# Fused FFT-attention and Mamba layers on one core: the diagonals of B go through DRAM

## The chip, the core and the metric

The kernel runs on one core of a Trainium2 chip. The metric is the device time of one execution in microseconds (us); the result of a version is the median of several runs. The core has a matrix engine (PE, whose weight loads are listed as PEld), three other compute engines (DVE, ACT, POOL) and SP, which here only issues transfers. Transfers run on 16 DMA engines that all queues share.

## The reference

Two layers act on x of shape 8 x 128 x 128 x 128 (batch, channel, height, width). Layer 0, a block of FFT attention and convolutions, isn't touched by the change. Layer 1 is a selective state-space scan over the 16384 pixels of each image (`_gn` is a group norm):

```python
x = x + _L1_conv_ref(_gn(x), ...)

xz = u @ W_in                                  # u: pixels x 128 channels
xs, z = jnp.split(xz, 2, axis=-1)              # 256 inner channels each
xc = jax.nn.silu(depthwise causal conv of xs, 4 taps)
dt, Bm, Cm = jnp.split(xc @ W_xproj, [8, 24], axis=-1)   # 8, 16 and 16 columns
delta = jax.nn.softplus(dt @ W_dt + b_dt)
A = -jnp.exp(A_log)
def step(hs, inp):
    d_t, B_t, C_t, u_t = inp
    dA = jnp.exp(d_t[:, :, None] * A)
    h_new = dA * hs + (d_t * u_t)[:, :, None] * B_t[:, None, :]
    y_t = jnp.einsum('bdn,bn->bd', h_new, C_t)
    return (h_new, y_t)
y = ys + xc * D_param;  y = y * silu(z);  out = y @ W_out
```

Each image has 256 x 16 states (inner channel x state index n). For each pixel, a state is multiplied by dA and gets delta * xc * B added.

## The kernel before

Layer 0 runs first and leaves x1 in DRAM. After line 1020 the scan part follows. It cuts each image into 32 chunks of T = 512 pixels (`NCH`), 256 chunks in all, and each chunk into 16 steps (`ST`). One step handles 32 inner channels and, on the 128 partitions, 4 groups q of state indices; within a group two of the four indices m (`mp` says which pair) lie side by side. `where(n)` splits the step number n into chunk i, half h of the inner channels, pair mp and block k: steps 0 to 3 and 8 to 11 of a chunk use mp = 0, the others mp = 1.

A step passes four engines:

- `decay` (ACT): dA = exp(A * dlrep), twice, 128 x 512. `dlrep` holds the step sizes delta, repeated over the state groups. It is issued three steps ahead (`LEAD`).
- `product` (PE): hb = (delta * xc) * B for 128 rows and 2 x 512 columns, one step ahead, as 32 small matmuls. The weights are `duT`, the transposed delta * xc. The moving operand is `bd`: for each block j of 128 pixels, group q and pair mp a matrix that holds B on the diagonal of 64 pixels and zeros elsewhere, so that the matmul spreads the product over the pixels. hb lies in PSUM, with two buffers.
- `scan` (DVE): two tensor_tensor_scan over 512 pixels, reading dA and hb, writing `hs` (four buffers). ACT then copies the last column to `state` (`keep_state`).
- `weigh` (POOL): hc = hs * crep, where `crep` holds C repeated over 32 rows; `add` (PE) sums the groups into y.

Beside these, each chunk prepares the next ones. The list `beside` names, for every step, further pieces of work and the chunk that they are for (relative to i); `first` holds two that go ahead of the decay. They are the convolution and input projection (`conv`, `gate`, `xproj`), the step sizes (`step_sizes`, `step_sizes_act`), delta * xc (`drive`, on POOL) and its transpose (`turn`, `turn_act`), and the output (`skip`, `gated`, `project`, `residual`). `InOrder` holds PE, DVE, ACT and POOL to the order in which the program issues. SP's transfers aren't held so: the framework places them by its own estimate of when each is ready, and a transfer waits on SP, ahead of all that is issued later.

The columns of B take this way: `xproj_act` (step 5, for the next chunk) copies dt, B and C to `dbl`. `turn_b` (step 7) transposes the B rows on PE into a PSUM bank, so that pixels lie on the partitions; `keep_b` (step 8) copies them to `bt` on DVE. From step 11 on, `diagonals` makes a part of `bd` with one DVE product of `same` (an identity of 64, twice) and the transposed B, six such parts per chunk; `more_diagonals` makes the remaining 16 rows on ACT with `bt` as scale. `bd` has two buffers, one for each mp.

On SP, each chunk stores C (`cd`) to DRAM and reads it back repeated (`crep`, four transfers for each mp, `repeat_c`), and stores delta (`dld`) and reads it back repeated (`dlrep`, four transfers for each half h, line 1161). Every eighth chunk also loads an image block of 2 MB (`acc<-X`, `rows_of`) in pieces of 128 bytes, and ACT's queue stores one (`out<-acc`, `residual`).

Of the kernel before, what the change touches and what calls it, by code (L numbers as in the profile page):

```python
# [9 lines left out]
F32 = mybir.dt.float32  # L10
# [17 lines left out]
T = 512  # L28
# [83 lines left out]
def _layout(a):  # L112

    a = {n: np.asarray(v) for n, v in a.items()}
    o = {"x": np.ascontiguousarray(a["x"]).reshape(B, C, HW)}
    o["consts"], o["bconsts"], o["ker"] = _constants()
    p = "L0_conv_"
    f, s = a[p + "projf_w"].reshape(C, 2 * C), a[p + "projs_w"].reshape(C, 2 * C)

    rows = np.arange(C).reshape(2, 4, 16).transpose(1, 0, 2).reshape(-1)  # L120

    j, h = np.arange(8)[:, None], np.arange(NH)[None, :]
    frows = np.concatenate([(HD * h + j).reshape(-1), (HD * h + 15 - j).reshape(-1)])
    ws = [a[p + n + "1_w"].reshape(C, C) for n in "qkv"] + [f[:, frows], f[:, C:], s[:, rows], s[:, C:]]
    o["wpack"] = np.concatenate([w.T for w in ws] + [a[p + "w1"].reshape(NK, C).T], 1)
    tf = np.repeat(a[p + "temp_f"].reshape(NH), HD)
    ts = np.repeat(a[p + "temp_s"].reshape(NH), HD)[rows]
    o["cvec"] = np.stack([a[p + n + "1_b"] for n in "qkv"] + [tf, ts], 1)
    o["bn"] = np.concatenate([a[p + n] for n in ("b1", "bn_gamma", "bn_beta", "bn_mean", "bn_var")])[None]
    w2 = np.zeros((13, NK + 1, 13, C), np.float32)  # L130
    for u in range(13):
        w2[u, :NK, u] = a[p + "w2"].reshape(C, NK).T
        w2[u, NK, u] = a[p + "b2"]

    w2 = w2.reshape(13, NK + 1, 13, C // 8, 2, 4).transpose(0, 1, 4, 3, 5, 2)
    o["w2blk"] = w2.reshape(13 * (NK + 1), 13 * C)


    taps = np.zeros((4, NG, 2, 8, 8, 2, 4, 4), np.float32)
    for n, c in enumerate("qkvc"):  # L140
        for y in range(4):
            for x in range(4):
                taps[n, :, :, y + 1 : y + 4, x + 1 : x + 4, 0, y, x] = a[p + c + "3_w"]
                taps[n, :, :, y : y + 5, x : x + 5, 1, y, x] = a[p + c + "5_w"]
    taps = taps.reshape(4, NG // 4, 4, 2, 2, 4, 2, 4, 32)
    o["taps"] = taps.transpose(2, 3, 5, 7, 1, 0, 4, 6, 8).reshape(128, -1)
    p = "L1_conv_"
    o["win"] = a[p + "W_in"]
    o["cw"] = a[p + "conv_w"].T.reshape(1, 4 * DI)

    xp = a[p + "W_xproj"].reshape(2, 128, DR + 2 * DS).transpose(1, 0, 2)
    wx = np.zeros((128, 2, 4, 32), np.float32)
    wx[:, :, :2, :DR] = xp[:, :, None, :DR]
    wx[:, :, 2, :] = xp[:, :, DR:]
    o["wx"] = wx.reshape(128, 256)
    o["wdt"] = np.zeros((128, 128), np.float32)
    for h in range(2):
        o["wdt"][32 * h : 32 * h + DR] = a[p + "W_dt"][:, h * 128 : (h + 1) * 128]
    o["same64"] = np.tile(np.eye(64, dtype=np.float32), (2, 1))
    o["gath"] = np.tile(np.eye(32, dtype=np.float32), (4, 1))  # L160
    o["wout"] = a[p + "W_out"].reshape(2, 128, C).transpose(1, 0, 2).reshape(128, -1)
    halves = [a[p + n].reshape(2, 128).T for n in ("conv_b", "b_dt", "D_param")]
    o["dvec"] = np.concatenate(halves, 1)

    o["alog"] = a[p + "A_log"].reshape(DI // 32, 32, 4, 4).transpose(2, 1, 3, 0).reshape(128, -1)
    return {n: np.ascontiguousarray(v) for n, v in o.items()}
# [24 lines left out]
def tile_kernel(ctx: ExitStack, tc: tile.TileContext, I: dict, out: bass.AP):  # L191
# [830 lines left out]
    NQ, NM, NR, NBK = 4, 4, 32, DI // 32  # L1022
    ND, NTB = 64, T // 128
    QR = 32
    with tc.tile_pool(name="e_c", bufs=1) as cp, tc.tile_pool(name="e_w", bufs=2) as wk, tc.tile_pool(
        name="e_h", bufs=4
    ) as hp, tc.tile_pool(name="e_d", bufs=3, space=DRAM) as dp, tc.tile_pool(
        name="e_b", bufs=2, space=PSUM
# [4 lines left out]
            return t  # L1033

        gath = fixed("gath", [128, NR], I["gath"])
        same = fixed("same", [128, ND], I["same64"])
        unit = fixed("unit", [128, 128], I["consts"][:, 0:128])
        win = fixed("win", [128, 2 * DI], I["win"])
        wx = fixed("wx", [128, 2, 128], I["wx"])
        wdt = fixed("wdt", [128, 128], I["wdt"])  # L1040
        wout = fixed("wout", [128, 2, C], I["wout"])
# [3 lines left out]
        nc.scalar.activation(A, A, AF.Exp)  # L1045
        nc.vector.tensor_scalar(A, A, -1.0, None, ALU.mult)  # L1046

        wf = cp.tile([128, 4, DI], F32, name="wf")
        nc.sync.dma_start(wf.rearrange("p a d -> p (a d)"), I["cw"].partition_broadcast(128))
        for k in range(4):  # L1050
            nc.vector.tensor_tensor(wf[:, k, :], wf[:, k, :], win[:, 0:DI], ALU.mult)
        state = cp.tile([128, NM, NBK], F32, name="state")
        ch = {}
        total = B * NCH
        RT = T // W
# [3 lines left out]

        def load(i):  # L1060
            b, k = divmod(i, NCH)
            xin = wk.tile([128, T], F32, name="xin")
            nc.sync.dma_start(xin, X1[b, :, k * T : (k + 1) * T])
            ch[i] = {"xin": xin}

# [45 lines left out]
        def gate(i):  # L1111
            c = ch[i]
            c["sz"] = wk.tile([128, 2, T], F32, name="sz", bufs=3)
            for h in range(2):
                ps = bank("e_z", h)
                pe.matmul(ps, lhsT=win[:, DI + h * 128 : DI + (h + 1) * 128], rhs=c["u"][:, 3:], start=True, stop=True)
                act.activation(c["sz"][:, h, :], ps, AF.Silu)

        def xproj(i):
# [29 lines left out]
        def step_sizes_act(i):  # L1149
# [5 lines left out]
            nc.sync.dma_start(d.rearrange("h p t -> p h t"), c["dl"])  # L1155
            for h in range(2):
                if h:
                    repeat_c(i, 1)
                t = c["dlr", h] = wk.tile([128, 4, T], F32, name="dlrep")
                for q in range(NQ):  # L1160
                    nc.sync.dma_start(t[q * NR : (q + 1) * NR], d[h].rearrange("(k r) t -> r k t", r=NR))
# [29 lines left out]
                pe.transpose(c["bp"][:, 32 * j : 32 * j + 32], c["dbl"][rs, j * 128 : (j + 1) * 128], unit[rs, rs])  # L1191

        def keep_b(i):
            c = ch[i]
            c["bt"] = wk.tile([128, NTB, DS], F32, name="bt")
            dve.tensor_copy(c["bt"], c["bp"][:, : NTB * 32].rearrange("p (j n) -> p j n", n=32)[:, :, :DS])

        def diagonals(i, mp, j):


            c = ch[i]
            if (mp, j) in ((0, 0), (1, 0)):
                c["bd", mp] = wk.tile([128, NTB, NQ, ND, 2], F32, name="bd")
            to = [128, NQ, ND, 2]
            b = c["bp"][:, 32 * j : 32 * j + DS].rearrange("p (q m) -> p q m", m=NM)[:, :, 2 * mp : 2 * mp + 2]
            dve.tensor_tensor(
                c["bd", mp][:, j], same.unsqueeze(1).unsqueeze(3).to_broadcast(to), b.unsqueeze(2).to_broadcast(to), ALU.mult
            )

        def more_diagonals(i, which):  # L1210

            c = ch[i]
            for n in which:
                j, q, m = 2 + n // 8, n // 2 % 4, n % 2
                at = NM * q + 2 + m
                act.activation(c["bd", 1][:, j, q, :, m], same, AF.Identity, scale=c["bt"][:, j, at : at + 1])


        ST = 16
# [11 lines left out]
        def decay(n):  # L1231
            i, h, mp, k = where(n)
            for j in range(2):
                dA = hp.tile([128, T], F32, name="dA", bufs=10)
                kk = 4 * h + k
                act.activation(dA, ch[i]["dlr", h][:, k, :], AF.Exp, scale=A[:, 2 * mp + j, kk : kk + 1])
                dAs[n, j] = dA
# [69 lines left out]
        def residual(i):  # L1307
# [10 lines left out]

        beside = [
            (0, 1, lambda i: conv(i, 1, 2)),  # L1320
            (0, 0, lambda i: diagonals(i, 1, 1)),
            (0, 0, lambda i: more_diagonals(i, range(6, 11))),
            (1, 1, lambda i: conv(i, 1, 3)),
            (1, 0, lambda i: more_diagonals(i, range(11, 16))),
            (2, 1, conv_act),
            (2, -1, lambda i: add(i, 3, 0, 1)),
            (3, -1, lambda i: skip(i, 1)),
# [2 lines left out]
            (5, 1, xproj_act),  # L1330
            (5, 0, lambda i: add(i, 0, 0)),
            (6, 0, lambda i: add(i, 0, 1)),
            (6, 1, step_sizes),
            (6, 2, norm),
            (7, 1, turn_b),
            (8, -1, project),
            (8, 1, lambda i: drive(i, 0)),
            (8, 1, keep_b),
            (9, -1, residual),
            (9, 1, lambda i: drive(i, 1)),  # L1340
            (9, 2, lambda i: conv(i, 0, 0)),
            (10, 0, lambda i: add(i, 1, 0, 1)),
            (11, 0, lambda i: skip(i, 0)),
            (11, 1, lambda i: diagonals(i, 0, 0)),
            (11, 1, lambda i: turn(i, 0)),
            (11, 2, lambda i: conv(i, 0, 1)),
            (12, 0, lambda i: gated(i, 0)),
            (12, 1, lambda i: turn_act(i, 0)),
            (12, 1, lambda i: diagonals(i, 0, 1)),
            (12, 2, lambda i: conv(i, 0, 2)),  # L1350
            (13, 1, lambda i: diagonals(i, 0, 2)),
            (13, 1, lambda i: turn(i, 1)),
            (13, 2, lambda i: conv(i, 0, 3)),
            (14, 1, lambda i: turn_act(i, 1)),
            (14, 1, lambda i: diagonals(i, 0, 3)),
            (14, 0, lambda i: add(i, 2, 0, 1)),
            (15, 1, lambda i: diagonals(i, 1, 0)),
            (15, 1, lambda i: more_diagonals(i, range(6))),
            (15, 2, lambda i: conv(i, 1, 0, 1)),
        ]  # L1360
        first = [
# [46 lines left out]
```

## Time and profile before

| | before |
|---|---|
| median of 3 runs | 18559.42 us (18539.3 to 18562.05) |
| profiled execution | 18481.4 us, its span 18479.6 us |
| mean granted clock of PE | 0.958 |
| busy PE, DVE, POOL, ACT | 89%, 77%, 71%, 65% of the span |
| SP's hardware queue | 1730850 packets, 2206 MB, 43.9% of 16 engines |
| scans (DVE) | 1269 ns each |
| hc (POOL) | 2377 ns each |
| dA (ACT) | 714 ns each |

The shares are means over layer 0 (the first 14 of 40 slices) and the scan part (the rest), which have little in common. A row of a group gives engine, operation, output<-inputs, shapes and count; behind the first bar its busy time and the mean duration of one in ns; behind the second the idle time ahead of it and what ended that. In a row of SP's timeline the columns are start, time that the issuing took, queue, line, operation, transfer and count. In a row of waits they are engine, tile, what it waited for, us in total, number of times and the longest.

### The profile page before, as it was taken

The numbers are of one execution on the slowest core, as the hardware profiler recorded it, in microseconds if no ns is written. First come the engines' busy times: TensorE is split into PE (matmuls) and PEld (weight loads), VectorE is DVE, ScalarE is ACT, GpSimd is POOL, SyncE is SP. The second block draws the span as 40 slices with busy tenths as digits, with TensorE's granted clock in tenths as the row PEclk, the third lists the DMA queues.
The fourth block names the chain that finished last, engine by engine and source line by source line (L and its number), as shares of the span: only waits on it lengthen the run. The fifth ranks groups of instructions, "written<-read, shape, count | busy, mean of one in ns | idle before, by whom it ended". The sixth has DMA issues, their size and how long they took to land.

```text
span 18479.6 us, 790974 instructions
## 1 busy us (share of the span) xinstructions
PE 16503.3 (89%) x353336; PEld 9529.9 (52%) x353336; DVE 14244.2 (77%) x15987; ACT 12009.6 (65%) x26077; POOL 13090.9 (71%) x7572
## 2 busy tenths in 40 slices
PE   7789988888888889999999999999999999999998
PEld 5566665566555544444444444444444444444444
DVE  5544544334444479999999999999999999999999
ACT  4443434334233358778778878888888878887887
POOL 3333334444222269999999999999999989998998
PEclk8889999988999999999999999999999999999999
DMA  9963337777776654444454445444544454445443
GB/s 375 371 235 89 96 106 248 240 230 218 207 204 192 186 139 100 103 96 100 97 105 101 100 96 108 99 99 98 106 98 99 100 103 100 99 98 105 98 98 88
DMA packets 2434566, 2601.34 MB, mean 141 GB/s; under 512 B 1221965, under 2 KB 1624013, under 8 KB 2396866
## 3 DMA queue, kind: packets, MB, share of 16 engines
q1 hardware_dynamic: 1730850, 2206.28, 43.9%
q10 hardware_dynamic: 679840, 277.32, 7.1%
q0 software_dynamic: 20480, 67.13, 1.1%
q8 instruction: 2783, 45.60, 1.1%
q14 instruction: 613, 5.02, 0.1%
HBM read 1715.23 MB, written 834.93 MB: 138 GB/s over the span
## 4 chain that ended last, share of the span: by engine, by line
PE 56%; DVE 22%; DMA 8%; issue 7%; ACT 6%; POOL 1%; SPq 1%; DVEq 0%; ACTq 0%; POOLq 0%
DVE hs L180 15%; PE hb L180 14%; PE y L180 8%; PE c_mm L180 6%; PE e_xc L180 4%; DVE bd L180 3%; PE e_z L180 3%; PE e_x L180 3%; PE d_b L180 2%; PE a_mm L180 2%; DMA d_of<-OFL 2%; PE c_gram L180 2%; PE d_p L180 2%; DMA X<-d_x 2%; ACT L180 2%
## 5 line engine op out<-in xcount | busy, mean ns | idle before, releaser
L180 POOL TENSOR_TENSOR hc<-hs,crep 128x1024 f32<-128x1024 f32 x4096 | 9653.4, 2377 | 982.4 <-DVE hs L180 858.1
L180 DVE TENSOR_TENSOR_SCAN hs<-dA,state,hb 128x512 f32<-128x512 f32 x7936 | 9611.4, 1269 | 558.2 <-PE hb L180 418.8
L180 PEld LDWEIGHTS hb<-bd,duT 64*32 64x32 f32 x262144 | 3727.5, 106 | 3971.3 <-issue 2808.4
L180 PE MATMUL hb<-bd,duT 64*32 64x128 f32 x262144 | 4919.3, 275 | 798.9 <-issue 417.8
L180 ACT ACTIVATE dA<-dlrep,A 128x512 f32<-128x512 f32 x8192 | 5443.8, 714 | 59.6 <-DMA dlrep<-dld 51.6
L180 PE MATMUL e_xc<-u,wf 128*128 128x512 f32 x4096 | 2263.9, 646 | 34.1 <-DVE A L1046 20.8
L180 PE MATMUL y<-hc,gath 128*32 128x512 f32 x16384 | 2053.4, 601 | 32.5 <-issue 31.2
L180 ACT COPY state<-hs 128x2 f32<-128x2 f32 x4096 | 775.9, 189 | 1676.2 <-DVE hs L180 1649.5
L180 ACT ACT_TABLE_LOAD x1057 | 1356.1, 1283 | 75.0 <-PE e_dt L180 40.1
L180 PE MATMUL c_mm<-src,taps 32*32 32x512 f32 x32768 | 1211.5, 626 | 191.8 <-issue 158.7
L180 DVE COPY vst<-c_mm 128x512 f32<-128x512 f32 x1024 | 685.0, 689 | 717.4 <-PE c_mm L180 620.6
L180 ACT ACTIVATE bd<-same,bt 128x64 f32<-128x64 f32 x4096 | 1054.0, 339 | 0.8 <-PE hb L180 0.8
L180 DVE TENSOR_TENSOR bd<-same,e_bt 128x512 f32<-128x512 f32 x1536 | 1036.7, 675 | 0.0
L180 PEld LDWEIGHTS c_mm<-src,taps 32*32 32x32 f32 x32768 | 681.2, 105 | 683.7 <-issue 493.5
L180 POOL TENSOR_SCALAR qm<-vst,cst 128x512 f32<-128x512 f32 x256 | 505.4, 2070 | 745.4 <-DVE vst L180 745.2
L180 ACT ACTIVATE junk<-vst 128x256 f32<-128x256 f32 x1024 | 416.4, 410 | 923.0 <-DVE vst L180 921.9
L180 PE MATMUL a_mm<-xt,wp 128*128 128x256 f32 x3072 | 760.6, 409 | 264.5 <-ACT pk L180 184.1
L180 POOL TENSOR_TENSOR eo<-eo,et 128x1008 f32<-128x1008 f32 x128 | 298.8, 2334 | 969.3 <-DVE et L180 960.8
L180 POOL DMA_DIRECT2D X<-d_x x256 | 139.1, 543 | 1069.5 <-DVE d_x L180 939.9
L180 PEld LDWEIGHTS e_xc<-u,wf 128*128 128x128 f32 x4096 | 654.7, 194 | 440.2 <-issue 436.1
L180 DVE TENSOR_TENSOR d_x<-d_p,d_x 128x512 f32<-128x512 f32 x256 | 274.9, 1074 | 780.3 <-DMA d_x<-in_x 490.0
L180 PEld LDWEIGHTS a_mm<-xt,wp 128*128 128x128 f32 x3072 | 619.3, 205 | 421.7 <-ACT pk L180 194.6
(179 smaller groups left out, 20011.2 us busy)
## 6 DMA issues: line engine op xcount, KB each, us to landing
dlrep<-dld SPq DMA_DIRECT2D x2048, 256.0 KB
crep<-cd SPq DMA_DIRECT2D x2048, 128.0 KB
dld<-dl SPq DMA_DIRECT2D x256, 512.0 KB
src<-Pq SPq DMA_DIRECT2D x128, 544.5 KB
src<-Pv SPq DMA_DIRECT2D x128, 544.5 KB
src<-Pk SPq DMA_DIRECT2D x128, 544.5 KB
src<-Px SPq DMA_DIRECT2D x128, 544.5 KB
xt<-in_x SPq DMA_DIRECT2D x64, 1024.0 KB
```

What stands on the lines that cost most here:

```text
L180: made = method(*args, **kwargs)
```

## The change

`bd` is no longer made by DVE and ACT. At the start of the scan part four DRAM buffers (`diag`, two for alternating chunks times two for mp, 1 MB each) are filled with zeros from a zeroed tile. `keep_b`, now in step 6 and on ACT, copies the transposed B to `bt` and issues four transfers on SP, each of which writes 64 x 16 pieces of two numbers (8 bytes) from `bt` onto the diagonals of the DRAM buffers; the zeros between stay. `load_b` reads a whole buffer of 1 MB back as `bd`. Both loads of a chunk are issued in `step_sizes_act`, after the four repeats of the first half of the step sizes, ahead of `crep` of mp = 1 and the second half. `bd` has three buffers now. To make room, the first half of `win` is kept only until `wf` is made from it, `xin` has one buffer, and `dA` nine instead of ten. `turn_b` moves from step 7 to step 6, ahead of `step_sizes`.

```diff
+    cp = ctx.enter_context(tc.tile_pool(name="e_c", bufs=1))
+    wf = cp.tile([128, 4, DI], F32, name="wf")
+    nc.sync.dma_start(wf.rearrange("p a d -> p (a d)"), I["cw"].partition_broadcast(128))
+    DROW = NTB * NQ * ND * 2
+    diag = {(n, mp): dram.tile([128, DROW], F32, name=f"diag{n}{mp}") for n in range(2) for mp in range(2)}
+    with tc.tile_pool(name="e_0", bufs=1) as zp:
+        win_x = zp.tile([128, DI], F32, name="win_x")
+        nc.sync.dma_start(win_x, I["win"][:, 0:DI])
+        for k in range(4):
+            nc.vector.tensor_tensor(wf[:, k, :], wf[:, k, :], win_x, ALU.mult)
+        zero = zp.tile([128, DROW], F32, name="zero")
+        nc.gpsimd.memset(zero, 0.0)
+        for d in diag.values():
+            nc.sync.dma_start(d, zero)
...
-            xin = wk.tile([128, T], F32, name="xin")
+            xin = wk.tile([128, T], F32, name="xin", bufs=1)
...
             for h in range(2):
                 if h:
+                    load_b(i, 0)
+                    load_b(i, 1)
                     repeat_c(i, 1)
                 t = c["dlr", h] = wk.tile([128, 4, T], F32, name="dlrep")
...
         def keep_b(i):
             c = ch[i]
-            c["bt"] = wk.tile([128, NTB, DS], F32, name="bt")
-            dve.tensor_copy(c["bt"], c["bp"][:, : NTB * 32].rearrange("p (j n) -> p j n", n=32)[:, :, :DS])
-        def diagonals(i, mp, j):
...
-        def more_diagonals(i, which):
...
+            bt = wk.tile([128, NTB, DS], F32, name="bt")
+            act.copy(bt, c.pop("bp")[:, : NTB * 32].rearrange("p (j n) -> p j n", n=32)[:, :, :DS])
+            for mp in range(2):
+                d = diag[i % 2, mp]
+                for x in range(2):
+                    ap = [[DROW + 2, ND], [2 * ND, NTB * NQ], [1, 2]]
+                    to = bass.AP(d.tensor, d.offset + x * ND * DROW, ap)
+                    frm = bt[ND * x : ND * x + ND].rearrange("p j (q m) -> p (j q) m", m=NM)[:, :, 2 * mp : 2 * mp + 2]
+                    nc.sync.dma_start(to, frm)
+
+        def load_b(i, mp):
+            t = ch[i]["bd", mp] = wk.tile([128, NTB, NQ, ND, 2], F32, name="bd", bufs=3)
+            nc.sync.dma_start(t.rearrange("p j q t m -> p (j q t m)"), diag[i % 2, mp])
...
-                dA = hp.tile([128, T], F32, name="dA", bufs=10)
+                dA = hp.tile([128, T], F32, name="dA", bufs=9)
...
         beside = [
-            (0, 0, lambda i: diagonals(i, 1, 1)),
-            (0, 0, lambda i: more_diagonals(i, range(6, 11))),
-            (1, 0, lambda i: more_diagonals(i, range(11, 16))),
...
+            (6, 1, turn_b),
             (6, 1, step_sizes),
+            (6, 1, keep_b),
             (6, 2, norm),
-            (7, 1, turn_b),
-            (8, 1, keep_b),
...
-            (11, 1, lambda i: diagonals(i, 0, 0)),
-            (12, 1, lambda i: diagonals(i, 0, 1)),
-            (13, 1, lambda i: diagonals(i, 0, 2)),
-            (14, 1, lambda i: diagonals(i, 0, 3)),
-            (15, 1, lambda i: diagonals(i, 1, 0)),
-            (15, 1, lambda i: more_diagonals(i, range(6))),
```

## The prediction

> **What bounds the kernel now.** I read the page's slices first: from slice 16 on (the scan part, about 11.9 of 18.5 ms) DVE, PE and POOL all stand at 9 tenths, so no single busy share names the bound. The change touches only this part, so I then read one ordinary chunk and one disturbed one. The timeline of SP's queue cuts the chunks: the store of the step sizes (`dld<-dl`) goes out once per chunk.
>
> ```profile
> 10109.19 0.78 SPq L1131 DMA_DIRECT2D cd<-dbl  x2
> 10111.23 0.34 SPq L1063 DMA_DIRECT2D xin<-X  x1
> 10111.74 2.17 SPq L1140 DMA_DIRECT2D crep<-cd  x4
> 10114.01 0.38 SPq L1155 DMA_DIRECT2D dld<-dl  x1
> 10117.56 1.74 SPq L1161 DMA_DIRECT2D dlrep<-dld  x4
> 10126.23 1.71 SPq L1140 DMA_DIRECT2D crep<-cd  x4
> 10128.03 2.65 SPq L1161 DMA_DIRECT2D dlrep<-dld  x4
> ```
>
> The next `dld<-dl` stands at 10159.22: 45.2 us. Over all 256 chunks this distance is mostly 44.6 to 45.2, except every eighth, in which an image block of 2 MB is stored and the next one loaded in 128-byte pieces: 10338.47 to 10390.52, 52.1 us. So 224 ordinary chunks and 32 block chunks. The stretches of both:
>
> ```profile
> 10109.00:10154.00 45.00, 42.08 (x1136) 22.02 (x1136) 44.03 (x43) 37.30 (x81) 42.84 (x21) 1.00 0.36 92
> 10338.00:10390.00 52.00, 43.56 (x1123) 22.50 (x1130) 43.87 (x42) 37.05 (x80) 42.17 (x21) 0.97 1.03 162
> ```
>
> Columns: length, busy PE, PEld, DVE, ACT, POOL, granted clock, DMA share, GB/s. In the ordinary chunk DVE is busy 44.0 of 45.0 and sets the pace; but POOL (42.8) and PE (42.1) are only 1.2 and 2.0 behind. In the block chunk the engines do the same work and 7 us are lost. The groups between 10 and 14 ms (86.5 chunks) price the work, and PE's waits in the two stretches say what it lacks:
>
> ```profile
> L180 DVE TENSOR_TENSOR_SCAN hs<-dA,state,hb 128x512 f32<-128x512 f32 x2704 | 3273.8, 1268 | 195.2 <-PE hb L180 146.8 <-ACT bd L180 17.6 <-POOL hc L180 13.1
> L180 POOL TENSOR_TENSOR hc<-hs,crep 128x1024 f32<-128x1024 f32 x1383 | 3259.5, 2377 | 329.4 <-DVE hs L180 281.0 <-DMA dlrep<-dld 14.2 <-PE e_z L180 11.1
> L180 PE MATMUL hb<-bd,duT 64*32 64x128 f32 x88576 | 1663.1, 275 | 262.3 <-issue 143.2 <-DVE hs L180 117.0
> L180 ACT ACTIVATE bd<-same,bt 128x64 f32<-128x64 f32 x1376 | 354.0, 339 | 0.0
> L180 DVE TENSOR_TENSOR bd<-same,e_bt 128x512 f32<-128x512 f32 x516 | 347.3, 673 | 0.0
> ```
>
> ```profile
> PE hb L180 <- DVE hs L180: 1.2, 2, 0.7
> PE hb L180 <- issue: 1.2, 1, 1.2
> PE e_o L180 <- ACT dl L180: 0.5, 1, 0.5
> ...
> PE hb L180 <- issue: 4.2, 3, 2.6
> PE y L180 <- issue: 2.8, 1, 2.8
> ```
>
> The first three are the ordinary chunk, the last two the block chunk. "Issue" is time in which PE waited for nothing that the profile shows. It is 1.2 us in the one and 7.0 in the other, and the DMA share is what differs (0.36 against 1.03). In the block chunk the two long stalls begin, within 0.2 us, when a 16 KB packet of the instruction queue is under way. I read them as instruction fetches delayed by traffic; that reading is inferred.
>
> **What goes.** Per chunk six DVE products (6 x 0.673 = 4.0 us) and DVE's copy of bt (0.2); 16 ACT diagonals (16 x 0.339 = 5.4). DVE falls to 44.0 - 4.2 = 39.8 us of need and stops being the bound; ACT was not one. What is late next: POOL needs 42.8. PE needs 42.1 + 0.5 (e_o on ACT) + its issue stalls; with the 1.2 of today, 43.8. So PE, not POOL, comes next, and at unchanged stalls an ordinary chunk gains the 1.2 us that PE now waits for DVE, no more.
>
> A rule of the Trainium skill speaks against taking PE so: Perfetto Trace Analysis, Identifying the Most-Contended Engine, holds matmul busy time a poor measure of PE's headroom and asks for the share of weight loads; the row gives 22.02 of 45 us, under half. By that rule PE has room, POOL's 42.8 binds, and the 224 ordinary chunks could give 2.2 us each, some 490 us. I go by PE's timeline, which between 10126 and 10134 shows back-to-back matmuls.
>
> **What comes, on PE.** Two loads of 1 MB in 8 KB pieces. The first 30 us of the kernel, loads and stores of such pieces, moved 12.17 MB at 97.3% of the engines: 2.1 MB are 5.0 us. Four writes of 1024 pieces of 8 bytes, 256 pieces per DMA engine. No row has 8-byte pieces; the nearest are the 128-byte ones:
>
> ```profile
> q10 hardware_dynamic: 16400, 2.10, 62.4%
> ...
> q1 hardware_dynamic: 16310, 2.43, 155.1%
> ```
>
> The block store: 62.4% of 16 engines for 25 us over 16400 packets, 15.2 ns; the block load: 155.1% over 16 us, 24.3 ns (overlapping). Far ends: half of 15.2, and the 70 ns of the mean packet of SP's queue (39.6% over 4000 us, 362592 packets). I take 15.2, the write to DRAM: 3.9 us per chunk (2 to 18). The Trainium skill (DMA: Bandwidth & Descriptors, Measured) has 10.5 ns per packet in a minimum-size transfer; by it the writes would be 2.7 us, an estimate that no run here shows.
>
> Stalls per us of DMA time: ordinary 1.2 per 16.2 (0.07); the excess of the block chunk 5.8 per 37.4 (0.16). At these rates the additions cost 5.0 x 0.07 + 3.9 x 0.16 = 1.0 us more stall, nearly the whole 1.2. A stall beside another wait costs nothing, so I take 0.8: an ordinary chunk gains 0.4 us (bounds: 1.2 gained with no added stall, 0.3 lost with pieces at 24 ns and more stall per piece). 224 x -0.4 = **-90 us**.
>
> **What comes, on SP and the step sizes.** In the built order SP now issues cd, crep, the four diagonal writes, dld, the first diagonal load, the first-half dlrep, the second load, crep, the second-half dlrep. So the first load stands ahead of both halves, and its wait for the first two writes to land holds up the first half. With t0 the cd issue: crep is issued to 4.2, the writes add 4 x 0.43 = 1.7, dld goes at about 6.0 (now 4.8). Its data stand behind the small pieces, which start about 0.7 after their first issue: 5.3 + 3.9 + 1.3 = 10.5, seen at 11.7 (1.2 of latency, an estimate: today's 3.55 from dld to dlrep, less 0.38 to issue and 1.3 to move, leaves 1.9 for both ends). dlrep is issued then (now 8.4), its four issues take 1.74, its data go behind the load's 2.5 us and have landed about t0 + 17. It is needed by dA of the next chunk at 10126.72, t0 + 17.5; really late only when PE lacks duT, which ACT makes 3.4 us later, for the product at 10132.74: t0 + 20.1. So 3 us to spare, gone at 27 ns per small piece; beyond that each further 10 ns adds 2.6 us to every chunk. At 15.2 ns: nothing.
>
> The diagonals themselves are needed at t0 + 23.5 and land by about 14. The second load waits for PE's last product of step 11, but the crep behind it waits for POOL's step 11 anyway, and what follows is used 6 steps later: nothing. One xin buffer (freed 10 steps before), nine dA (ACT waits for the same scan's state copy first), e_bt ahead of e_dt on PE and the bt copy on ACT (0.4 and 0.2 us, inside the spare): nothing.
>
> **The block chunk.** The block store starts at t0 + 9.0 and holds half of every engine for 15.6 us. Already now ACT waits 2.2 us there for dlrep, to t0 + 19.7, and is saved by the spare. After: issue 3.3 later plus the load's 2.5 us at half rate, 8.3 later in all: t0 + 28, 7.9 too late; part of that falls into stalls that are there anyway. I take +6.5 (0 to 10): 32 x 6.5 = **+208 us**.
>
> **The start.** 4 MB of zeros and a memset go ahead of the constants: 4.2 MB at 12.17 MB per 29.2 us is 10 us, while the first block load, 16 us, moves behind the first xin. +10 (-10 to +30).
>
> **Sum**: -90 + 208 + 10 = +128 on the profiled execution's own 18481.4 us. The median of the runs shown, 18559.4, is 78 above that; with the same difference 18,690 us.
>
> **Rivals.**
> 1. Faster: the instruction fetches do not mind the new traffic, ACT's lead of three steps hides the late dlrep. For it: DVE alone holds the pace in ordinary chunks. Against it: 7 us of stall in the block chunk. Price: 224 x -1.0 + 32 x 2 + 0 = -160 to 18,400; with POOL the only bound 18,070.
> 2. Much slower: the 8-byte pieces take 40 ns and the first load blocks SP. Place: dlrep of the first half, every chunk; it decides from 27 ns on. Price: arrival 6.3 later, 3.3 too late; 224 x 2.9 + 32 x 12.5 + 10 = +1060, 19,620. For it: these are the smallest pieces of the kernel; against it: both 128-byte rows lie below 27.
> 3. No change: gain and losses cancel, 18,560; the sum's three terms are of one size, so this is thin but real.
>
> **Chances.** My forecast, slower by 0.2 to 2% (18,600 to 18,930), 0.36; slower than that, with rival 2 at its end, 0.24; rival 1 0.31; rival 3 0.09. A difference under 0.2% can't be told from none here. The range leaves out the POOL-bound end and pieces beyond about 37 ns: 18,300 to 19,500.
>
> **What would show it.** DVE's bd group gone and DVE near 88% of an ordinary chunk; PE's issue waits up from 1.2 to about 2 us per chunk; dlrep issued 3 us later after cd than now; block chunks at 58 us instead of 52. Wrong if SP waits long at the first load (rival 2: ACT waits for dlrep in every chunk), or if ordinary chunks come out below 44 us (rival 1).

## The result and the profile after

| | before | after |
|---|---|---|
| median of 4 runs each | 18549.36 us | 19732.94 us (19723.83 to 19737.89) |
| ratio | 1 | 1.064, 95% interval 1.0622 to 1.0658 |
| span of the profiled execution | 18479.6 us | 19722.0 us |
| mean granted clock of PE | 0.958 | 0.938 |
| ordinary chunk, mean | 45.42 us | 49.90 us |
| block chunk, mean | 52.33 us | 59.45 us |
| SP's hardware queue, share of 16 engines | 43.9% | 56.9% |

The kernel is 6.4% slower; 0.7% was forecast. The place is clear: 224 ordinary chunks x 4.48 us = 1003 us, 32 block chunks x 7.12 = 228, and the first `dld<-dl` comes 16 us later. These add to 1247 us; the spans differ by 1242.

SP's timeline of one ordinary chunk after the change:

```profile
10120.02 0.78 SPq L1141 DMA_DIRECT2D cd<-dbl  x2
10121.98 1.72 SPq L1150 DMA_DIRECT2D crep<-cd  x4
10123.79 3.79 SPq L1217 DMA_DIRECT2D diag<-bt  x4
10127.68 0.60 SPq L1165 DMA_DIRECT2D dld<-dl  x1
10130.06 0.34 SPq L1221 DMA_DIRECT2D bd<-diag  x1
10134.04 1.76 SPq L1173 DMA_DIRECT2D dlrep<-dld  x4
10136.23 1.24 SPq L1221 DMA_DIRECT2D bd<-diag  x1
10137.52 2.10 SPq L1150 DMA_DIRECT2D crep<-cd  x4
10140.64 6.57 SPq L1173 DMA_DIRECT2D dlrep<-dld  x4
```

The four diagonal writes occupy SP for 3.79 us (1.7 were forecast), so `dld` goes out 7.7 us after `cd`, and the first half of the repeats 14.0 us after it. The next `cd<-dbl` is at 10169.27. The stretch of this chunk, with the columns of the stretches shown before (length, busy PE, PEld, DVE, ACT, POOL, granted clock, DMA share, GB/s):

```profile
10120.00:10169.00 49.00, 43.21 (x1136) 22.59 (x1131) 40.40 (x36) 32.73 (x64) 42.14 (x21) 0.97 0.59 128
```

DVE is down to 40.4 us as forecast, and it bought nothing: no engine is now busy for more than 43.2 of 49 us. The waits of the same stretch say what took its place:

```profile
DVE hs L179 <- PE hb L179: 7.9, 4, 3.4
ACT dA L179 <- DMA dlrep<-dld: 6.2, 1, 6.2
PE hb L179 <- issue: 4.8, 3, 2.3
...
PE e_o L179 <- ACT dl L179: 1.0, 1, 1.0
```

DVE now waits for PE's products. ACT waits 6.2 us for the repeated step sizes. PE waits 4.8 us, in three stalls, for nothing that the profile's semaphores show; it was 1.2. Below, such a wait is called an issue stall. The groups between 10 and 14 ms (78.3 chunks after, 86.4 before) show that this is the rule:

```profile
L179 DVE TENSOR_TENSOR_SCAN hs<-dA,state,hb 128x512 f32<-128x512 f32 x2436 | 2940.8, 1264 | 797.5 <-PE hb L179 558.3 <-ACT dA L179 146.5 <-POOL hc L179 31.5
L179 ACT ACTIVATE dA<-dlrep,A 128x512 f32<-128x512 f32 x2502 | 1660.2, 714 | 590.3 <-DMA dlrep<-dld 588.4
L179 PE MATMUL hb<-bd,duT 64*32 64x128 f32 x79968 | 1587.9, 281 | 416.3 <-issue 302.2 <-ACT duT L179 98.9 <-DVE hs L179 7.8
L179 PE MATMUL y<-hc,gath 128*32 128x512 f32 x4992 | 667.5, 629 | 34.5 <-issue 34.5
```

PE's wait for DVE went from 117.0 to 7.8 us in 4 ms, so the change took away what it set out to take away. "Issue" went from 143.2 to 302.2, a wait for `duT` (98.9) is new, and ACT's wait for `dlrep` is 588.4 where it was 14.7.

Some of PE's stalls cost more than their length. PE's timeline, with the wait in brackets:

```profile
10140.90 1.16 PE L179 MATMUL hb<-bd,duT 64*32 64x128 f32 x64
10141.99 1.92 PE L179 MATMUL y<-hc,gath 128*32 128x512 f32 x16
10146.17 1.70 PE L179 MATMUL hb<-bd,duT 64*32 64x128 f32 x64 [2.26 <-issue]
10147.80 3.04 PE L179 MATMUL e_xc<-u,wf 128*128 128x512 f32 x4
```

After a stall of 2.26 us the same 64 products take 1.70 us instead of 1.16. The stretches of the stall and behind it say why (the seventh column is the granted clock):

```profile
10144.00:10146.00 2.00, 0.00 (x0) 0.00 (x0) 0.67 (x1) 2.00 (x5) 2.00 (x2) 1.00 1.02 186
10146.20:10149.60 3.40, 3.40 (x66) 2.05 (x66) 1.58 (x2) 2.69 (x7) 1.29 (x1) 0.55 1.06 225
```

The granted clock halves for one stretch of 3.4 us. Over the scan part the clock stands at one half for 1256 us, before for 367; half of that time is counted as lost. Of the 1256 us, 846 follow issue stalls (311 before) and 362 follow waits of PE for `duT` (none before).

The packets of the instruction queue in the trace tell what ends the issue stalls. After the change PE has 437 of them over 1 us in the scan part, and 96% end 1.2 to 1.8 us after a 16 KB packet of that queue has ended; 10% of moments picked at random do, and 3% of PE's waits for `dl`. Before the change it is 99% of 194. So PE waits there for its next instructions. The packets take hardly longer than before (1.17 us on average, 1.15 before) but come late: the one that ends such a stall starts 7.6 us after the one ahead of it, where the median of all is 5.4.

The bill per chunk, averaged over all (46.28 us before, 51.09 after, +4.81), from the waits of PE in these 4 ms and the half-clock time of the whole scan part:

| on PE, us per chunk | before | after | |
|---|---|---|---|
| issue stalls (hb, y, e_xc) | 1.84 | 4.39 | +2.55 |
| half of the half-clock time (367 and 1256 us over 256 chunks) | 0.72 | 2.45 | +1.73 |
| hb waits for `duT` | 0 | 1.26 | +1.26 |
| e_o waits for `dl` | 0.42 | 0.89 | +0.47 |
| hb waits for DVE | 1.35 | 0.10 | -1.25 |
| sum | | | +4.76 |

(`e_o` is the output product; it uses a PSUM bank that ACT frees by reading it into `dl`, the step sizes delta. `duT` comes from ACT too, in order behind the dA.) The five lines make up nearly all of the 4.81 us. PE's own busy time bears out the second: 42.6 us per chunk before, 44.4 after.

### The profile page after: what moved, and what is told of

It reads as the page before. It is cut to its first block, busy times and chain, and to the rows that moved or that the text cites. A ratio compares the mean times of both kernels' runs of the same rounds, so it can differ in the third digit from the quotient of the medians.

```text
span 19722.0 us, 787877 instructions
## 1 busy us (share of the span) xinstructions
PE 16953.1 (86%) x353336; PEld 9662.7 (49%) x353336; DVE 13418.0 (68%) x14195; ACT 10974.1 (56%) x22237; POOL 13070.1 (66%) x7573
## 3 DMA queue, kind: packets, MB, share of 16 engines
q1 hardware_dynamic: 2870114, 2755.80, 56.9%
## 4 chain that ended last, share of the span: by engine, by line
PE 63%; DMA 15%; ACT 9%; issue 7%; DVE 4%; SPq 1%; POOL 1%; ACTq 0%; DVEq 0%; POOLq 0%; another core or an unknown queue 0%
PE hb L179 17%; PE e_xc L179 9%; PE y L179 8%; PE c_mm L179 6%; DMA dlrep<-dld 5%; DMA dld<-dl 4%; ACT dA L179 3%; PE e_z L179 2%; PE e_x L179 2%; DMA d_of<-OFL 2%; ACT L179 2%; PE d_b L179 2%; PE a_mm L179 2%; PE d_p L179 2%; PE c_gram L179 2%
## 5 line engine op out<-in xcount | busy, mean ns | idle before, releaser
L179 PE MATMUL hb<-bd,duT 64*32 64x128 f32 x262144 | 5201.8, 280 | 1376.8 <-issue 990.4
L179 PEld LDWEIGHTS hb<-bd,duT 64*32 64x32 f32 x262144 | 3864.0, 108 | 4778.0 <-issue 3106.9
L179 PE MATMUL e_xc<-u,wf 128*128 128x512 f32 x4096 | 2412.6, 685 | 50.0 <-issue 31.1
L179 PE MATMUL y<-hc,gath 128*32 128x512 f32 x16384 | 2168.0, 623 | 110.1 <-issue 108.6
L179 PEld LDWEIGHTS e_xc<-u,wf 128*128 128x128 f32 x4096 | 701.4, 207 | 524.1 <-issue 520.9
L179 PEld LDWEIGHTS y<-hc,gath 128*32 128x32 f32 x16384 | 426.6, 111 | 903.1 <-issue 850.1
```

What stands on the lines that cost most here:

```text
L179: made = method(*args, **kwargs)
```

## The experiments

Two theories were set against each other. Theory 1: the step sizes come late, because SP issues the writes and a load ahead of them. Theory 2: the new traffic stalls PE's instruction supply, and the stalls halve the clock. A third, that DVE's time is worth nothing, was tested beside them. All ratios are to the kernel before, run on the same chip; a point is 1% of its time. The summary first; waits are us in the 4 ms from 10 to 14 ms, half clock is us over the scan part. In the last four runs SP's order is held and the image block falls on two of eight chunks, so there the last column is the mean of the other six.

| run | ratio (95%) | PE hb issue wait | ACT dA wait for dlrep | half clock | ordinary chunk |
|---|---|---|---|---|---|
| before | 1 | 143 | 15 | 367 | 45.42 |
| after | 1.064 (1.062-1.066) | 302 | 588 | 1256 | 49.90 |
| e1_no_transfers | 0.978 (0.976-0.980) | 127 | 8 | 188 | 43.41 |
| e2_loads_only | 1.015 (1.014-1.017) | 255 | 33 | 747 | 46.31 |
| e3_writes_only | 1.011 (1.009-1.013) | 191 | 394 | 498 | 45.86 |
| e14_delay_alone | 0.993 (0.992-0.995) | 113 | 375 | 403 | 44.31 |
| e16_loads_and_delay | 1.040 (1.037-1.043) | 238 | 416 | 1134 | 47.90 |
| e4_loads_behind | 1.069 (1.067-1.072) | 286 | 432 | 1364 | 49.20 |
| e5_writes_behind_dld | 1.080 (1.079-1.082) | 358 | 385 | 1701 | 50.27 |
| e13_writes_on_act | 1.089 (1.087-1.091) | 226 | 1 | 1938 | 51.46 |
| e11_before_held | 1.003 (1.002-1.004) | 148 | 7 | 390 | 45.30 |

### No transfers: what DVE's time is worth

The four writes and two loads go; both matrices are constant tiles with ones on the diagonals.

```diff
-                    nc.sync.dma_start(to, frm)
+                    pass
...
-            t = ch[i]["bd", mp] = wk.tile([128, NTB, NQ, ND, 2], F32, name="bd", bufs=3)
-            nc.sync.dma_start(t.rearrange("p j q t m -> p (j q t m)"), diag[i % 2, mp])
+            ch[i]["bd", mp] = bd_fixed[mp]
```

> Leaves out the diagonals of B altogether: no small writes, no loads, the product reads two tiles with ones on the diagonals, loaded once (its result is not the reference's). It shows what freeing DVE and ACT is worth without any new traffic. Theory 1 (the loss is the late step sizes: SP waits at the first load, and its data go ahead of the first half) and theory 2 (the loss is the traffic itself: PE's instruction supply stalls and its clock halves after the longer gaps) both expect a gain here: ordinary chunks at 43.4 to 43.8 us, 18,200 to 18,350 us in all. Theory 3 (DVE was not worth anything, PE or POOL hold the pace) expects 18,500 or more.

Measured: 18034.21 us, ratio 0.9782. The time that DVE and ACT no longer spend is worth 2.0 us per ordinary chunk, where the prediction had at most 1.2, and the whole time lies below the 18,200 to 18,350 expected. In 4 ms without the transfers PE, PEld, DVE, ACT and POOL are busy so:

```profile
10000.00:14000.00 4000.00, 3752.66 (x101719) 1948.37 (x101706) 3634.80 (x3146) 2997.94 (x5747) 3801.03 (x1801) 0.99 0.47 104
```

POOL, at 95%, is the busiest. Theory 3 falls. What the transfers cost is thus not 6.4 points but 8.6.

### One half of the transfers at a time

Loads without writes (the diagonals hold ones from the start), then writes without loads.

> The changed kernel without the small writes (the buffers hold constant ones; its result is not the reference's). As nothing is waited for, the first load stands on SP before the next cd, away from the step sizes; both 1 MB loads remain. Theory 1: no late step sizes, so ACT waits for dlrep under 0.5 us per chunk and the time is within 100 us of e1, below 18,450. Theory 2: PE's issue waits stay near 3 us per chunk and the time is 18,800 or more.

> The changed kernel without the loads (the product reads two constant tiles; its result is not the reference's); the four small writes stay ahead of dld. Theory 1: dlrep is issued about 2.5 us later than before after cd, still inside its spare, so within 150 us of e1. Theory 2: the 4096 small pieces stall PE's supply by about 1 us per chunk: 18,500 to 18,700.

Measured: 18722.78 us (1.0154) and 18639.63 us (1.0109). The loads alone cost 3.7 points over e1 and double PE's issue waits, with the step sizes nearly on time (33 us). That is theory 2, though the time stays a little below its 18,800. The writes alone cost 3.3 points and show both: issue waits up by half, and 394 us of ACT waiting for `dlrep`. The time lies nearer theory 2's number, but this run can't part the two. The framework placed the loads otherwise than in the change (one ahead of `cd`, one behind the first half of the repeats), since they had no writes to wait for.

### Late without traffic, and traffic with lateness

e1, with eight writes of 16 rows in the place of the diagonal writes: SP is occupied a little longer (4.5 us; the diagonal writes take 3.2 in the median chunk of the writes-only run), 32 KB go in 128 pieces instead of 4096.

```diff
-                for x in range(2):
-                    ap = [[DROW + 2, ND], [2 * ND, NTB * NQ], [1, 2]]
...
+                for x in range(4):
+                    nc.sync.dma_start(d[16 * x : 16 * x + 16, 0 : NTB * DS], bt[16 * x : 16 * x + 16].rearrange("p j n -> p (j n)"))
```

> No small pieces and no loads, as in the run without transfers (ratio 0.978); in the place of the four diagonal writes SP issues eight writes of 16 rows of 256 bytes (32 KB in all), which take it 3 to 4 us and move almost nothing. So the step sizes are as late as in the run with the writes alone (1.011), without its traffic. If late step sizes are what costs (theory 1): 1.00 to 1.01, with ACT waiting for dlrep some 400 us in 4 ms. If the traffic costs (theory 2): 0.978 to 0.985, and PE's issue waits stay at 127 us in 4 ms. Between the two: the shares of both.

Measured: 18341.16 us, 0.9932 [0.9917, 0.9947], between the two. Its waits from 10 to 14 ms:

```profile
ACT dA L179 <- DMA dlrep<-dld: 375.2, 86, 16.0
...
PE hb L179 <- issue: 113.2, 100, 3.2
...
PE hb L179 <- ACT duT L179: 71.9, 45, 11.1
```

The wait for `dlrep` is the one of the writes-only run, PE's issue waits are not raised, and PE waits for `duT` in half of the chunks. So lateness by itself costs 1.5 points (0.9932 - 0.9782), and the 8-byte pieces 1.8 more (1.0109 - 0.9932). Theory 1 is right for nearly half of what the writes cost. Lateness also halves the clock: 403 us here against 188 in e1, and 133 of them follow waits for `duT`. In the median chunk `dld` went out 4.2 us later after `cd` than in e1 (9.1 against 4.9), the first half of the repeats 12.7 after `cd`, and the next chunk's first dA ran at 20.5 instead of 16.8. In the writes-only run it ran at 21.4, so the 1.8 points hold a little lateness too.

The same eight writes put into the loads-only run:

> The loads-only run (1.0154) with eight writes of 16 rows of 256 bytes ahead of dld: 3 to 4 us of SP's time, no small pieces. Delay alone cost 0.015 on the run without transfers. If delay and traffic add: 1.028 to 1.034. If they make each other worse (the repeats wait behind the loads' data): 1.035 to 1.05. If the loads hide the delay: below 1.025.

Measured: 19271.88 us, 1.0399 [1.0373, 1.0425]. The parts would add to 1.030; 0.9 points more came, with an uncertainty of some 0.4: lateness costs more beside the loads. PE's waits (10 to 14 ms) show where:

```profile
PE hb L179 <- issue: 238.2, 146, 5.1
PE hb L179 <- ACT duT L179: 91.6, 34, 9.2
```

The issue stalls are not longer than with the loads alone (254.6). What came is the wait for `duT`, which the loads-only run doesn't have, and half-clock time: 747 us with the loads alone, 1134 here, 355 of them behind waits for `duT`. From the whole change this run still differs by 1.064 - 1.040 = 2.4 points. They hold the 8-byte pieces, but also the place of the first load: here it stands behind the first half of the repeats and waits for no write; in the change it stands ahead of them, and the first dA comes at 24.2 instead of 21.1. No run parts these two.

### By which way the loads slow PE

e1 with two copies of 1 MB per chunk from DRAM to DRAM: nothing is written to the on-chip tiles, no product waits.

```diff
             ch[i]["bd", mp] = bd_fixed[mp]
+            nc.sync.dma_start(copies[i % 2, mp], diag[i % 2, mp])
```

> As the run without transfers (0.978), and per chunk two copies of 1 MB from DRAM to DRAM in the place of the two loads: the same bytes read by the same DMA engines, nothing written to the tiles that the engines use, and no product waits for them. If the loads cost by holding up PE's instruction supply in the DMA engines or DRAM: near the loads-only run, 1.005 to 1.02, PE's issue waits near 250 us in 4 ms. If they cost by writing to the on-chip memory or because a product waits for bd: 0.978 to 0.988, issue waits near 127 us.

Measured: 18787.92 us, 1.0142 [1.0117, 1.0167]: the loads-only run's 1.0154. PE's issue wait, copies first, loads second:

```profile
PE hb L179 <- issue: 257.8, 177, 3.8
```

```profile
PE hb L179 <- issue: 254.6, 151, 4.4
```

So it isn't the writing into on-chip memory, and not a product that waits for `bd`. In the run with the copies 99% of PE's 364 issue stalls over 1 us end 1.2 to 1.8 us after an instruction packet, as in the change. What is left is that these packets are held up in the DMA engines or in DRAM; which of the two, no run shows.

Half of the loads:

> The loads-only run (1.0154) with one of the two 1 MB loads per chunk, the other matrix constant; no writes. If the loads' cost goes by their traffic: about half of the way from 0.978 to 1.0154, 0.992 to 1.001, PE's issue waits near 190 us in 4 ms. If it is the load that stands among the step sizes on SP: the kept load is that one, and the time stays near 1.01 to 1.0154.

Measured: 18366.37 us, 0.9914 [0.9892, 0.9936], issue wait 184 us. One load costs 1.3 points over e1, two cost 3.7: more than in proportion. The premise of the second theory didn't hold, since the framework put the remaining load behind the second half of the repeats; the run says that traffic in a quieter place is cheaper, or that load costs grow faster than bytes, and can't part these.

Loads in pieces of 2 KB instead of 8:

> As e2 (loads only, constant ones on the diagonals; its result is not the reference's), with each row of 8 KB cut into four pieces of 2 KB. If instruction fetches wait behind single large pieces, PE's issue waits fall from 3.3 to below 2.4 us per chunk and the ratio to 1.00 or less. If the moved bytes or the time that the DMA engines are busy decide, it stays at 1.01 to 1.02.

Measured: 18770.82 us, 1.0141, as with 8 KB. Smaller pieces between which a fetch could slip in don't help.

The busy share of the DMA engines over one ordinary chunk in 40 slices, before and then after, shows what "traffic" means here:

```profile
DMA  0117989039996000883999700000000000000000
```

```profile
DMA  0069545999998999999999999820000000000000
```

Before, the transfers come in three bursts with holes. After, the holes are filled and the engines stand at 8 tenths or more for 19 slices of 1.2 us on end, 23 us, and the repeats of the step sizes are in the midst of it. The mean share (0.36 and 0.59 of the engines' time) hides that.

### Mending SP's order

SP is held to the order of the program, so that both loads really go between the two halves; in a second run the small writes also go behind `dld`; in a third they go to ACT's queue instead.

```diff
+        sp = InOrder(tc, nc.sync)
...
-                    nc.sync.dma_start(to, frm)
+                    act.dma_start(to, frm)
```

> The changed kernel whole, with SP's transfers of the scan part held to the order in which the program issues them, so that both loads of diagonals really stand between the two halves of the step sizes. Theory 1: ACT's wait for dlrep falls from 7.5 us per chunk to under 1 and the time to 18,600 to 18,900. Theory 2: PE's issue waits (4.4 us per chunk) and the halved clock stay, the time stays above 19,400.

> The changed kernel whole, SP's transfers held to the program's order, and the four small writes issued after dld instead of ahead of it; the loads stand behind the first half of the step sizes. Theory 1 now says: not the loads but the small writes ahead of dld make the step sizes late, and that is what the two additions cost together beyond e2 and e3 apart (about 300 us) and some more. It expects dlrep back at 9 to 10 us after cd, ACT's wait for it under 1 us per chunk, and a ratio to before of 1.035 to 1.045. Theory 2 (stalls of PE's instruction supply by the traffic, wherever it stands) expects 1.055 or more.

> The whole change with the loads held behind the first half of the repeats (ratio 1.069 with the writes on SP), and the four diagonal writes issued on ACT's queue instead of SP's. The traffic is the same; SP issues dld and dlrep about 3.7 us earlier, ACT spends about as much on issuing. If SP's time is what costs (theory 1): 1.02 to 1.04, ACT's waits for dlrep under 150 us in 4 ms. If the traffic costs (theory 2): 1.055 to 1.07, PE's issue waits still near 285 us in 4 ms. ACT, busy 33 of 49 us, should bear the 3.7 us, though they delay whatever ACT does behind them.

> The kernel before, with SP held to the order in which the program issues, and nothing else: the control for the runs that hold SP so. If holding costs nothing: 0.998 to 1.002, and those runs may be set beside the change as it is. If holding costs by itself (a transfer that waits blocks what stands behind it): 1.003 to 1.015, and their ratios contain that much that isn't the change's.

Measured: 1.0693, 1.0804, 1.0892 and, for the control, 1.0029 [1.0018, 1.0039]. Holding the order costs 0.3 points by itself, so the first three may be read as about 1.066, 1.077 and 1.086, if it adds. None helps. SP's order with the writes behind `dld`:

```profile
10133.03 0.77 SPq L179 DMA_DIRECT2D cd<-dbl  x2
10135.06 1.71 SPq L179 DMA_DIRECT2D crep<-cd  x4
10137.93 0.38 SPq L179 DMA_DIRECT2D dld<-dl  x1
10138.36 3.66 SPq L179 DMA_DIRECT2D diag<-bt  x4
10142.26 3.00 SPq L179 DMA_DIRECT2D dlrep<-dld  x4
10145.96 2.31 SPq L179 DMA_DIRECT2D bd<-diag  x2
```

Here `dlrep` goes out 9.2 us after `cd`, where the kernel before had 8.4, and ACT still waits 385 us in 4 ms for it; the first dA runs at 20.6. Issued early isn't landed early; that its data share the engines with the small pieces and the loads is the likely reason, but not shown. PE's issue waits are the highest of all runs (358). With the loads held back, PE also waits for `bd` (128 us in e4, up to 10.7 us at a time, and 99 in e5). That a denser bunch of transfers is what makes e5 worse than e4 fits the issue waits, but was only argued.

With the writes on ACT's queue the wait for `dlrep` is gone (1.3 us in 4 ms). PE's timeline shows what took its place:

```profile
10127.55 2.16 PE L179 MATMUL hb<-bd,duT 64*32 64x128 f32 x128
10135.30 3.78 PE L179 MATMUL e_o<-yt,wout 128*128 128x512 f32 x4 [5.58 <-ACT dl L179]
```

ACT issues the four writes in 4.38 us, ahead of `dl`; PE stands in order before e_o, whose buffer `dl` frees, for 359.8 us in 4 ms, 4.7 per chunk, and the clock halves behind it (e_o took 3.78 us for four products of 0.63; 1451 of the run's 1938 us at half clock follow these waits). So this run removes one lateness and makes another, and is no clean test of theory 1.

### Fewer pieces

The run with the writes behind `dld`, with one piece of 128 bytes per pixel instead of sixteen of 8, so 256 instead of 4096; `bd` is laid out to match.

```diff
-                    ap = [[DROW + 2, ND], [2 * ND, NTB * NQ], [1, 2]]
+                    ap = [[DROW + 32, ND], [1, 32]]
...
-                    rhs=bd[rs, j, q],
+                    rhs=bd[rs, :, j, q],
```

> As e5, but the columns of a diagonal lie together: one piece of 128 bytes per pixel in place of 16 pieces of 8, so 256 small pieces per chunk instead of 4096; the loads stay 1 MB each, and PE reads its moving operand with a stride. If the number of pieces is what the writes cost, the ratio falls to that of the loads alone (1.015 to 1.025). If PE pays for the stride, the hb matmuls get longer than 280 ns. If the cost is in the four transfers and their landing rather than in the pieces, the ratio stays within 0.01 of e5.

Measured: 19561.37 us, 1.0570, 2.3 points below its partner e5, with a product at 291 ns instead of 283. That is near the 1.8 and 2.4 of the other pairs, but like them it isn't the pieces' traffic alone: SP issues the four writes in 2.6 instead of 3.7 us, and ACT's wait for `dlrep` falls from 385 to 166 us in 4 ms. It misses the 1.015 to 1.025 that was expected if the pieces' number were the main matter: PE still has 264 us of issue stalls and waits 96 us for `bd`.

### A way that is faster than both kernels

If DVE paces the kernel before and DMA isn't free, then ACT, busy 37 of 45 us, can take some of DVE's products without any transfer. One and then two of the six products of DVE are made by ACT, row by row:

```diff
+        def rows_on_act(i, j, which):
+            c = ch[i]
+            for n in which:
+                q, m = n // 2, n % 2
+                at = NM * q + m
+                act.activation(c["bd", 0][:, j, q, :, m], same, AF.Identity, scale=c["bt"][:, j, at : at + 1])
...
+            (11, 1, lambda i: rows_on_act(i, 3, range(0, 2))),
+            (12, 1, lambda i: rows_on_act(i, 3, range(2, 5))),
+            (13, 1, lambda i: rows_on_act(i, 3, range(5, 8))),
-            (14, 1, lambda i: diagonals(i, 0, 3)),
```

> The kernel before, without any new transfer: one of DVE's six diagonal products per chunk is made by ACT instead, as eight rows in steps 11 to 13, where ACT waits for the scans. DVE loses 0.67 us per chunk, ACT gains 2.7 and stays at about 40 of 44 us. If DVE sets the pace of ordinary chunks, as read from the profile of before, they fall by 0.4 to 0.6 us: a ratio of 0.990 to 0.995. If PE or POOL set it, no change.

> The kernel before, with two of DVE's six diagonal products made by ACT as 16 rows in steps 11 to 14 (eight rows gave 0.995). DVE loses 1.35 us per chunk, ACT gains 5.4 - of which it has room for, being busy 37 of 45 us. If DVE sets the pace with PE 1 to 2 us behind: 0.990 to 0.995. If ACT's rows now come late for PE or delay the dA (ACT as the next bound): 0.996 to 1.01.

Measured: 18423.52 us, 0.9948 [0.9932, 0.9965], and 18317.18 us, 0.9918 [0.9903, 0.9933]. Both are as expected, and the second beats both kernels. PE's wait for DVE falls from 117 to 83 and 74 us in 4 ms; ACT is then busy for 3550 of 4000 us.

## Why the prediction was wrong

The direction was right; the size was not. By the prediction's own steps:

- **DVE falls to 39.8 us and stops being the bound.** Right: 40.4, and PE's wait for it went from 1.35 to 0.10 us per chunk. The value was set too low: "the 1.2 us that PE now waits for DVE, no more" is 2.0 in e1. Averaged over all chunks e1 gains 1.78: the wait for DVE gives 1.32, the clock 0.35, issue stalls 0.21, e_o takes 0.59 back, and the remaining 0.5 stands in PE's own busy time (42.6 us a chunk before, 41.7 in e1). The rule of the Trainium skill that the prediction set against its own (Perfetto Trace Analysis, Identifying the Most-Contended Engine) would have given 2.2 us per ordinary chunk with POOL as the bound. With the transfers out of the way that is nearer to the 2.0 measured than the prediction's 1.2, and POOL is the busiest engine of e1; that POOL binds there isn't shown, since PE is at 94% beside its 95.
- **1.0 us more PE stall per chunk.** The step that failed first: 2.55 more. The rate per us of DMA time was taken from a mean share (0.07 in ordinary chunks), and the new transfers don't fall into mean conditions: they fill the holes between the old ones (that this is why the rate fails fits the half-loads run, but isn't shown by itself). The prediction's guess that the stalls are late instruction fetches was right. The two loads alone raise the stalls by 1.7 us a chunk (hb, y and e_xc: 1.63 in e1, 3.37 in e2), where the prediction had 5.0 x 0.07 = 0.35.
- **No term for the clock.** The prediction counted a stall as its own length. The added half-clock time costs 1.73 us per chunk, 443 us in all, more than a third of the loss; it follows the issue stalls and the waits for `duT` alike.
- **The step sizes: nothing, 3 us to spare.** The arrival was wrong by 7 us, in three places: the writes take SP 3.4 us in the median chunk, 3.8 in the one shown, and not 1.7 (`dld` at 7.9 after `cd` in the median chunk, not 6.0); `dld` takes 6.9 us until the repeats can go, not 5.7 (14.8, not 11.7); and from there to the first dA it is 9.4, not 5.3 (24.2, not 17). The limit that the prediction gave, 20.1, is passed by 4 us, and was if anything too late: with dA at 20.5, e14 already loses 0.9 us per ordinary chunk. In the change PE's wait for `duT`, put at nothing, is 1.26 us per chunk, and the 362 us at half clock behind it cost another 0.7.
- **An 8-byte piece at 15.2 ns.** Right: the 256 pieces of an engine went from 6.0 to 10.4 us after `cd`, 17 ns each. The 2.7 us that the prediction sets beside it doesn't follow from the page it cites: the 10.5 ns there are the time of a whole transfer over its 64 packets, not one engine's time for a piece, and the run shows 4.4 us. Rival 2 set its threshold by this price, and so looked for the danger in the wrong number.
- **Block chunk +6.5 us; start +10.** Near: +7.1 and +16. For the block chunk this is partly luck: the forecast gave the whole of it to late step sizes, but PE's wait for `duT` is 1.7 us of a block chunk (the mean of 31); the half-clock loss grew by 2.0 us and the issue stalls by 1.7.
- **Rivals.** Rival 2 (late step sizes in every chunk, 19,620) comes closest to the 19,733 measured, and the wait that it named is there: ACT waits for `dlrep` in every chunk. But its mechanism is at most half of what happened: the pieces take 17 ns and not 40, and SP's wait at that load is 87 us in 4 ms, 1.1 per chunk. The load does add to the lateness (first dA at 24.2, without the loads 21.4), but lateness by itself is 1.5 points of the 8.6 that the transfers cost. Rival 1's gain is real only without the transfers. The high end of the range, 19,500, left out that a late arrival and more traffic could both hold.

In points of the time before, the runs divide the 6.4 so: -2.2 for what DVE and ACT no longer do (e1), +3.7 loads (e2 - e1), +1.5 lateness (e14 - e1), +0.9 lateness and loads together (e16), +2.4 small pieces and the first load's place among the repeats (after - e16). Each difference is uncertain by some 0.3, the 0.9 by 0.4. The loads of e2 and e16 stand elsewhere on SP than in the change, so the parts are those of these runs, not the change's own. What stays open: whether the instruction packets wait in the DMA engines or in DRAM, how much of the 2.4 is the pieces, and why the writes behind `dld` are worse than ahead of it.

## What to carry to other kernels

Work moved from an engine to DMA wasn't free in this kernel, where PE runs some 1100 small products per chunk and its instructions come by DMA: look at the DMA engines' share slice by slice, not at its mean, and price each new wait of PE, whatever its cause, with the half-clock stretch that may follow it. For a transfer on a critical chain, add the time that SP takes to issue what is ahead of it, and the data in flight when it lands; an early issue alone bought nothing. When one engine leads the others by only 1 to 2 us in 45, shifting two small products to an engine that has room gave 0.8%, and a whole new path lost 6.4.

## What the runs showed of the hardware

- PE's clock halves after gaps of 1.6 us and more, not always. In the kernel before, of the gaps in PE's records in the scan part, half clock followed 5% of those of 1.2 to 1.6 us (65 gaps), 38% of 1.6 to 2.0 (37), 52% of 2.0 to 2.5 (54) and 72% of 2.5 to 3.5 (40). Half-clock stretches are 3.4 us long, or multiples of it. The Trainium skill (TensorE: Matmul & The Clock Gate, HAM oscillation — how this bites in real kernels) gives as the rule that PE should have no idle gaps above about 3.4 us; here much shorter ones were enough.
- PE's issue stalls end with the instruction queue: 96 to 100% of those over 1 us end 1.2 to 1.8 us after a 16 KB packet of it has ended (before, after, e1, e2, e14 and e15).
- A copy from DRAM to DRAM slows PE as much as a load into the tiles that it reads (1.0142 and 1.0154).
- SP took 0.9 us to issue a write of 1024 pieces of 8 bytes, 0.65 for 64 pieces of 128 (2.61 us for four) and 0.5 to 0.6 for 16 rows of 256 bytes (4.47 us for eight), so the time to issue grows little with the pieces. Under the added traffic the issuing of later transfers stretches: the four repeats of the second half took 6.57 and 9.25 us in two chunks after, 2.65 before.
